# Graph-layer kernel: more gathered tiles replaced by column copies, and the copies spread over ScalarE and three places of VectorE's step

## The chip, the cores and the metric

The kernel runs on one core of one Trainium2 chip. The metric is device time in microseconds from start to end of one execution. The engines are TensorE (PE, with PEld for its weight loads), VectorE (DVE), ScalarE (ACT), GpSimd (POOL) and SyncE (SP). Each has its own in-order queue, and semaphores order them between each other. In the profile a name with a trailing q (DVEq, ACTq) stands for an instruction that the engine's queue handles itself, such as a load of registers.

## What is computed

The reference is one message-passing layer on a graph with 12,500 nodes (64 features each) and 200,000 edges (32 features each), sorted by destination, followed by a residual and a layer norm:

```python
msg_in = concatenate([x[src], x[dst], edge_attr_32], axis=-1)        # 200000 x 160
messages = relu(msg_in @ mW1 + mb1) @ mW2 + mb2                       # 160 -> 128 -> 64
aggregated = segment_sum(messages, dst, num_segments=12500)
upd = relu(concatenate([x, aggregated]) @ uW1 + ub1) @ uW2 + ub2      # 128 -> 128 -> 64
out = layernorm(x + upd)                                              # float32, no scale or shift
```

## The kernel before

The edges are cut into 1563 tiles of 128, and six tiles make a step, so there are 261 steps (`NSUB`). Two steps form a super-step `g` of 12 tiles. The product with `mW1` is split into three parts by the rows of the matrix. The part for `x[src]` is made once for all nodes: a table A of 12,500 rows of 128 numbers in DRAM (`tab_a`). For each tile POOL gathers the 128 rows that belong to its edges with one indirect DMA (L207, into `xg`). The part for `x[dst]` plus the bias is a second table B, of which 32 consecutive rows (a window) are enough for a tile because the edges are sorted. The part for the edge features is multiplied directly.

A step `s` of the main loop then runs like this:

- `edge_part(s)` on PE, already issued during step s - 1: for each tile one matmul (L363; two passes each, so twelve in the profile) of the left operand `l` (edge features, and a 0/1 matrix that picks the window's row) with `rhs` (weights and window rows), into the PSUM tile `pc`.
- `node_part(s)`: DVE adds the gathered rows, `h = pc + xg` (L390, or L386 for four tiles), and ACT takes the ReLU in place (L391, or L387 and L388).
- `collect(s - 1)` on PE: each tile's `h` is multiplied with a 0/1 matrix `sel` and summed into `sums` (L418), and a count of edges is kept (L423).
- In even steps `select(g + 1)`: DVE makes the 0/1 parts of the next super-step's `l` (L233, L235) and its `sel` (L239); SP then loads the edge features into `l` (`load`, L254), and ACT makes a bfloat16 copy of `sel` (`counts`, L247). In odd steps SP loads destinations (`loadd`).
- When a range of up to 448 nodes is complete, the step is an update. There are 33 of them, at steps that lie 47 apart at first and 4 apart at the end, since the later edges belong to more nodes. `close` copies the sums (ACT, L437 and L438), `update` multiplies (PE, L460 and L461) and ACT takes a ReLU with a bias (L462), `residual` multiplies again (PE, L469 and L470), DVE takes statistics (`bn_stats`, L474 and L476), ACT a square root with a bias (L478), and `norm`, at the start of the next step, lets DVE write the result (L484, L487), which SP stores. `pc`, `pu` and `py` share two PSUM slots.

The buffers for gathered rows form a ring of nine steps: POOL may gather a step as soon as DVE has added the rows of the step nine before it.

**Copied tiles.** In some steps (the list `COPIED`) the last two of six tiles are not gathered. The node features lie transposed in SBUF instead, one node in a column: `xtop` has them in its upper 64 partitions and zeros below, `xbot` the other way round. For 128 edges of each of the two tiles a tile `xc` of 128 x 128 is put together column by column: the upper half of column e is the source node of edge e of the first tile, the lower half that of the second. PE multiplies it with the weights (L366, four matmuls of 64 rows) on top of `pc`. Which column to copy is known only at run time, so registers are loaded with the column numbers (`values_load_multi_w_load_instructions`, a TENSOR_LOAD in the queue) and the copies address SBUF through them. `copies(s)` runs at the end of each step and makes a fourth of the `xc` that is needed two steps after the last fourth:

- ACT makes columns 0 to 63 (`SINGLE`), each with two copies of 64 partitions, upper and lower (L328, L330); 16 columns a step, after one load of 16 registers that hold two numbers each.
- DVE makes columns 64 to 127, each with one bitwise OR of an `xtop` and an `xbot` column (L341); 16 a step, after one load of 32 registers (L334).

`COPIED` is 20, 24, ..., 248. In the main loop of the kernel before, the part that matters here is in this order (what is left out stands between):

```python
node_part(s); collect(s - 1); close(...)
if j == 0 and g + 1 < NSUP:
    select(g + 1); load(g + 1); counts(g + 1)
...
update(...); edge_part(s + 1); residual(...)
rest(s)
copies(s)
```

Nothing reorders it: each engine's queue holds its instructions in the order in which this loop writes them.

Of the kernel before, what the change touches and what calls it, by code (L numbers as in the profile page):

```python
# [10 lines left out]
F32 = mybir.dt.float32  # L11
I32 = mybir.dt.int32
# [5 lines left out]
P = 128  # L18
# [53 lines left out]
YBASE = XBASE + 4 * XCOLS  # L72
FIRST, GAPS = 20, (4,)
COPIED = []
while FIRST + sum(GAPS) * (len(COPIED) // len(GAPS)) + sum(GAPS[:len(COPIED) % len(GAPS)]) < NSUB - 12:
    COPIED.append(FIRST + sum(GAPS) * (len(COPIED) // len(GAPS)) + sum(GAPS[:len(COPIED) % len(GAPS)]))
RNDS = -(-len(COPIED) // len(GAPS))
SINGLE = 64

# [19 lines left out]
def gnn_kernel(ctx: ExitStack, tc: tile.TileContext, x1T, x, eT, e_rows, src, src_row, dst, dst_row, wlist, wrow, wnext, whalf,  # L99
# [41 lines left out]
    cols = const.tile([RNDS * len(GAPS), 2 * P], I32, name="cols")  # L141
    col_i = const.tile([RNDS * len(GAPS), SINGLE, 2], U16, name="col_i")
    col_a = const.tile([RNDS * len(GAPS), P - SINGLE, 2], I32, name="col_a")
    w1b = const.tile([P, DH], F32, name="w1b")
# [67 lines left out]
    with tc.tile_pool(name="sup", bufs=2) as sup, tc.tile_pool(name="work", bufs=2) as work, tc.manual_schedule():  # L212
# [12 lines left out]

        def select(g):

# [6 lines left out]
            for r in ([slice(0, P)] if g > 2 else [slice(q, q + WIN) for q in SK]):  # L234
                nc.vector.tensor_tensor(l[r], l[r].bitcast(I32),  # L235
                                        node[r].unsqueeze(2).broadcast_to([r.stop - r.start, SUP // 2, P]),
                                        op=ALU.is_equal)
            s = sup.tile([P, SUP, WIN], F32, name="sel")
            nc.vector.tensor_tensor(s[:, :nt], slot.unsqueeze(1).broadcast_to([P, nt, WIN]),  # L239
# [46 lines left out]
        def columns_list():  # L286

            for r in range(len(GAPS)):
                v = src_row[:, ((FIRST + sum(GAPS[:r])) * SUB + SUB - 2) * P:]
                nc.sync.dma_start(cols[r * RNDS:(r + 1) * RNDS],  # L290
                                  bass.AP(v.tensor, v.offset, [[sum(GAPS) * SUB * P, RNDS], [1, 2 * P]]))
            cv = cols.rearrange("k (b e) -> k b e", b=2)
            iv = col_i.rearrange("k (b e) h -> k b e h", b=2)
            nc.vector.tensor_scalar(iv[:, :, :, 0], cv[:, :, :SINGLE:2], 4.0, float(XBASE), op0=ALU.mult, op1=ALU.add)
            nc.vector.tensor_copy(iv[:, :, :, 1], cv[:, :, 1:SINGLE:2])
            for b, base in enumerate((XBASE, YBASE)):
                nc.vector.tensor_scalar(col_a[:, :, b], cv[:, b, SINGLE:], 4.0, float(base), op0=ALU.mult, op1=ALU.add)

# [6 lines left out]

        def copies(s):

            for j, c in enumerate(COPIED):
                gap = GAPS[(j - 1) % len(GAPS)]
                if c - 2 - gap <= s < c - 2:  # L310
                    break
            else:
                return
            q = s - (c - 2 - gap)
            k = j % len(GAPS) * RNDS + j // len(GAPS)
            if q == 0:
                xc[c] = work.tile([P, P], F32, name="xc")
            o8 = xc[c].bitcast(U8)
            last_a = 4 * (N - 1)
            lo, hi = shares(SINGLE, gap, 4)[q]  # L320
            _, v = nc.values_load_multi_w_load_instructions(  # L321
                col_i.rearrange("k e b -> k (e b)").bitcast(I32)[k:k + 1, lo:hi], engines=[ET.Activation],
                min_val=0, max_val=N * 65536 - 1, skip_runtime_bounds_check_because="sources are node numbers")
            for i, w in zip(range(lo, hi), v):
                b, e = divmod(i, SINGLE // 2)
                o = o8[b * D:b * D + D, 8 * e:8 * e + 8]
                n = (w & 65535).with_bounds(min_val=XBASE, max_val=XBASE + last_a) - XBASE
                nc.scalar.copy(o[:, :4], x8[:D, bass.ds(n, 4)])  # L328
                n = (w >> 16).with_bounds(min_val=0, max_val=N - 1) * 4
                nc.scalar.copy(o[:, 4:], x8[:D, bass.ds(n, 4)])  # L330
            lo, hi = shares(P - SINGLE, gap, 2)[q]
            for a in range(lo, hi, 16):
                m = min(a + 16, hi)
                _, v = nc.values_load_multi_w_load_instructions(  # L334
                    col_a.rearrange("k e b -> k (e b)")[k:k + 1, 2 * a:2 * m], engines=[ET.DVE], min_val=XBASE,
                    max_val=YBASE + last_a, skip_runtime_bounds_check_because="sources are node numbers")
                for e in range(a, m):
                    i, n = (w.with_bounds(min_val=base, max_val=base + last_a) - base
                            for w, base in zip(v[2 * (e - a):], (XBASE, YBASE)))
                    w = 4 * (SINGLE + e)  # L340
                    nc.vector.tensor_tensor(o8[:, w:w + 4], x8[:, bass.ds(i, 4)], y8[:, bass.ds(n, 4)],  # L341
                                            op=ALU.bitwise_or)

# [384 lines left out]
        for s in range(last + 2):  # L728
# [8 lines left out]
            if s < NSUB:  # L737
                node_part(s)
            if 1 <= s <= NSUB:
                collect(s - 1)  # L740
            if s + 1 in due:
                close(due[s + 1])
            if j == 0 and g + 1 < NSUP:
                select(g + 1)
                load(g + 1)
                counts(g + 1)
# [16 lines left out]
            rest(s)  # L763
            copies(s)
            if s - 1 in due:
# [171 lines left out]
```

## Time and profile before

| | us |
|---|---|
| median of 3 runs (lowest, highest) | 1831.2 (1829.88, 1834.96) |
| profiled execution | 1832.05 |
| its span, first to last instruction | 1830.3 |
| mean granted TensorE clock | 0.577 of full speed |

| engine | busy us | share of the span | instructions |
|---|---|---|---|
| PE | 1440.8 | 79% | 9446 |
| DVE | 856.1 | 47% | 4895 |
| ACT | 1157.8 | 63% | 8032 |
| POOL | 1369.6 | 75% | 1456 |

Register loads, waits and other work of a queue do not count as busy, so an engine with a low share may still be unable to start anything else. A group of the profile gives the line, the engine, the operation, its operands, how often it ran, its busy time and the mean in ns of one; then the idle time of the engine just before these instructions and what ended it. "issue" is idle time in which nothing that the profile shows was awaited. Copies on ACT and DVE overlap their neighbours, so their mean is longer than the distance between two of them.

### The profile page before, as it was taken

What the parts mean: (1) busy time and instruction counts of PE and PEld (TensorE: products, weight loads), DVE (VectorE), ACT (ScalarE), POOL (GpSimd) and SP (SyncE); (2) the same over time, 40 slices, a digit from 0 to 9 for tenths busy, and PEclk for the clock granted to TensorE, in tenths of its full rate; (3) what the DMA queues carried; (4) which work ended last, traced back from release to release, by engine and by line L of the source; (5) the groups of instructions that cost most, each with busy time, mean ns of one, the idle gap of its engine ahead of it and who ended that gap; (6) DMA issues with size and microseconds to landing.
All of it is one profiled execution on the core that took longest, in us unless ns stands there. A gap on an engine that the chain in (4) does not pass through costs nothing.

```text
span 1830.3 us, 51040 instructions
## 1 busy us (share of the span) xinstructions
PE 1440.8 (79%) x9446; PEld 1243.3 (68%) x9446; DVE 856.1 (47%) x4895; ACT 1157.8 (63%) x8032; POOL 1369.6 (75%) x1456
## 2 busy tenths in 40 slices
PE   3697897776777777777877788887888888888887
PEld 3586887676666666666766667776766766767765
DVE  1565664454444444435444445444444544544432
ACT  0224886676676767757766667676776776767511
POOL 7777777777777777777777777777777777777774
PEclk8755655555555555555555555555556556566565
DMA  8874444333333333333333333433343433444432
GB/s 212 202 147 123 125 125 120 96 90 91 90 93 94 95 91 94 101 92 98 100 100 102 99 102 100 107 104 100 106 106 101 110 103 101 109 107 108 109 103 63
DMA packets 209512, 197.52 MB, mean 108 GB/s; under 512 B 58284, under 2 KB 174079, under 8 KB 209199
## 3 DMA queue, kind: packets, MB, share of 16 engines
q0 software_dynamic: 46304, 92.96, 20.4%
q1 hardware_dynamic: 148350, 92.34, 18.5%
q10 hardware_dynamic: 14546, 8.93, 1.8%
q8 instruction: 90, 1.47, 0.3%
q14 instruction: 222, 1.82, 0.3%
HBM read 176.40 MB, written 17.66 MB: 106 GB/s over the span
## 4 chain that ended last, share of the span: by engine, by line
POOL 36%; issue 23%; PE 19%; DMA 10%; DVE 7%; ACT 3%; ACTq 1%; DVEq 1%; SPq 1%; POOLq 0%
POOL xg L207 36%; PE sums L418 7%; DMA xg<-tab_a,src_s 5%; PE pc L363 4%; DVE xc L341 2%; PE pu L460 2%; PE pu L461 1%; DMA tab_a<-tb 1%; DMA l<-in_dst_row 1%; DVE h L390 1%; DVE l L235 1%; PE py L469 1%; PE py L470 1%; ACTq L321 1%; ACT xc L328 1%
## 5 line engine op out<-in xcount | busy, mean ns | idle before, releaser
L207 POOL DMA_INDIRECT xg<-tab_a,src_s x1387 | 1310.8, 945 | 422.7 <-issue 402.0
L418 PE MATMUL sums<-sel,h 128*128 128x32 f32 x3126 | 665.9, 381 | 191.7 <-ACT h L391 186.7
L418 PEld LDWEIGHTS sums<-sel,h 128*128 128x128 f32 x3126 | 635.5, 307 | 254.5 <-ACT h L391 228.8
L328 ACT COPY xc<-xtop 64x4 uint8 x3712 | 698.4, 188 | 114.1 <-issue 112.8
L330 ACT COPY xc<-xtop 64x4 uint8 x3712 | 714.4, 192 | 10.9 <-issue 10.9
L363 PE MATMUL pc<-rhs,l 64*128 64x128 f32 x3126 | 421.5, 424 | 134.8 <-DVE o L487 113.4
L363 PEld LDWEIGHTS pc<-rhs,l 64*128 64x128 f32 x3126 | 349.9, 305 | 191.7 <-DVE o L487 117.1
L341 DVE TENSOR_TENSOR xc<-xtop,xbot 128x4 uint8 x3712 | 299.6, 155 | 278.4 <-issue 278.1
L390 DVE TENSOR_TENSOR h<-pc,xg 128x768 f32<-128x768 f32 (+1 forms) x194 | 183.6, 947 | 355.5 <-DMA xg<-tab_a,src_s 263.4
L391 ACT ACTIVATE h<-h 128x768 f32<-128x768 f32 (+1 forms) x194 | 162.2, 837 | 245.9 <-DVE h L390 235.4
L235 DVE TENSOR_TENSOR l<-l,cps 128x768 f32<-128x768 int32 (+1 forms) x134 | 127.8, 954 | 29.4 <-DMA l<-in_dst_row 25.1
L247 ACT CAST selb<-sel 128x384 bf16<-128x384 f32 x131 | 66.1, 505 | 68.0 <-DVE sel L239 62.0
L474 DVE BATCH_NORM_STATS2 st<-py 128x6 f32<-128x64 f32 x131 | 20.5, 218 | 145.0 <-PE py L470 141.7
L423 PE MATMUL cnt<-selb,one 128*1 128x32 bf16 x1563 | 84.8, 188 | 0.0
L239 DVE TENSOR_TENSOR sel<-cps,drc 128x384 f32<-128x384 f32 x131 | 71.9, 549 | 20.2 <-PE sums L418 19.3
L478 ACT ACTIVATE sd<-mv,eps 128x4 f32<-128x4 f32 (+1 forms) x33 | 9.8, 297 | 109.4 <-DVE mv L476 109.4
L207 POOL DMA_INDIRECT xg<-in_x,src_s x60 | 57.7, 962 | 19.1 <-issue 18.0
L423 PEld LDWEIGHTS <-one 128*1 128x1 bf16 x1563 | 54.0, 83 | 22.5 <-issue 8.7
L386 DVE TENSOR_TENSOR h<-pc,xg 128x512 f32<-128x512 f32 x58 | 39.8, 686 | 49.4 <-DMA xg<-tab_a,src_s 29.5
L460 PE MATMUL pu<-sums_s,w2u 128*128 128x448 f32 (+1 forms) x66 | 61.2, 1032 | 0.5 <-ACT sums_s L437 0.5
L469 PE MATMUL py<-ux,xw 128*128 128x64 f32 x262 | 54.0, 289 | 5.1 <-ACT hTu L462 4.9
L470 PE MATMUL py<-u,hTu 128*128 128x64 f32 x262 | 52.5, 283 | 0.4 <-ACT hTu L462 0.4
(105 smaller groups left out, 857.3 us busy)
## 6 DMA issues: line engine op xcount, KB each, us to landing
l<-in_dst_row SPq DMA_DIRECT2D x262, 96.0 KB
l<-in_eT SPq DMA_DIRECT2D x262, 96.0 KB
xg<-tab_a,src_s POOLq DMA_INDIRECT x1387
rhs<-tab_b SPq DMA_DIRECT2D x361, 32.0 KB
tab_b<-tb SPq DMA_DIRECT2D x13, 512.0 KB
rhs<-tab_b SPq DMA_DIRECT2D x387, 16.0 KB
tab_a<-tb ACTq DMA_DIRECT2D x12, 512.0 KB
out<-o SPq DMA_DIRECT2D x32, 128.0 KB
```

Source lines behind the costliest of these rows:

```text
L207: nc.gpsimd.indirect_dma_start(out=a[:, i, :] if s < XG else a[:, i // 2, i % 2, :], out_offset=None, in_=A[:, :] if s >= XG else x[:, :], ...
L235: nc.vector.tensor_tensor(l[r], l[r].bitcast(I32), node[r].unsqueeze(2).broadcast_to([r.stop - r.start, SUP // 2, P]), op=ALU.is_equal)
L328: nc.scalar.copy(o[:, :4], x8[:D, bass.ds(n, 4)])
L330: nc.scalar.copy(o[:, 4:], x8[:D, bass.ds(n, 4)])
L341: nc.vector.tensor_tensor(o8[:, w:w + 4], x8[:, bass.ds(i, 4)], y8[:, bass.ds(n, 4)], op=ALU.bitwise_or)
L363: nc.tensor.matmul(pc[:, b, k, :], L[g][q:q + 64, m, :], rhs[g % 2][q:q + 64, w, :], start=s >= XG or k == 0, stop=s >= XG and not copied)
L390: nc.vector.tensor_tensor(h[:, b, :m], pc[:, b, :m], a[:, b, :m], op=ALU.add)
L391: nc.scalar.activation(h[:, b, :m], h[:, b, :m], AF.Relu)
L418: nc.tensor.matmul(ps[:, bass.ds(ws[i], WIN)], h[:, i % 2, i // 2, :], S[g][:, k0 + i, :], start=False, stop=ends and i == n - 1)
L423: nc.tensor.matmul(pn[:, bass.ds(ws[i], WIN)], one, SB[g][:, k0 + i, :], start=False, stop=ends and i == n - 1)
L460: nc.tensor.matmul(pu, w2u, sums_s[u % 2][:, :n], start=True, stop=False)
L469: nc.tensor.matmul(py[:, i], xw[u % 2][:, i * P:(i + 1) * P], ux, start=True, stop=False)
```

## The change

- `COPIED` becomes 16, 19, 22, 24, 27, 30, 32, ..., 254: three copied steps in eight instead of two, and to nearer the end.
- ACT makes columns 0 to 55 (`ACTS`), each with a single ACTIVATE that adds the `xbot` column, as a pointer bias, to the `xtop` column (`singly`); 20, 20 and 16 in the steps of a gap of three, 28 and 28 in a gap of two. It stands right behind `node_part`, ahead of the step's other ACT work.
- DVE makes columns 56 to 127, still with one OR each, now on one 4-byte word instead of four bytes (`joined`); 24 a step in a gap of three, 36 in a gap of two. A step's share is cut into places: two in odd steps (behind `node_part`, at the end), three in even steps (behind `node_part`, within `select` between L235 and L239, at the end). Each place loads its own registers, at most 32 at once.

```diff
--- before.py
+++ after.py
@@ -70,12 +70,13 @@
 XBASE = 8320
 U8, U16 = mybir.dt.uint8, mybir.dt.uint16
 YBASE = XBASE + 4 * XCOLS
-FIRST, GAPS = 20, (4,)
+FIRST, GAPS = 16, (3, 3, 2)
 COPIED = []
-while FIRST + sum(GAPS) * (len(COPIED) // len(GAPS)) + sum(GAPS[:len(COPIED) % len(GAPS)]) < NSUB - 12:
+while FIRST + sum(GAPS) * (len(COPIED) // len(GAPS)) + sum(GAPS[:len(COPIED) % len(GAPS)]) < NSUB - 6:
     COPIED.append(FIRST + sum(GAPS) * (len(COPIED) // len(GAPS)) + sum(GAPS[:len(COPIED) % len(GAPS)]))
 RNDS = -(-len(COPIED) // len(GAPS))
-SINGLE = 64
+LAST = 4 * (N - 1)
+ACTS = 56
 
 
 def updates():
@@ -139,8 +140,8 @@
     past = const.tile([1, 1], F32, name="past")
 
     cols = const.tile([RNDS * len(GAPS), 2 * P], I32, name="cols")
-    col_i = const.tile([RNDS * len(GAPS), SINGLE, 2], U16, name="col_i")
-    col_a = const.tile([RNDS * len(GAPS), P - SINGLE, 2], I32, name="col_a")
+    col_i = const.tile([RNDS * len(GAPS), ACTS, 2], U16, name="col_i")
+    col_a = const.tile([RNDS * len(GAPS), P - ACTS, 2], I32, name="col_a")
     w1b = const.tile([P, DH], F32, name="w1b")
     b1 = const.tile([P, DH], F32, name="b1")
 
@@ -223,7 +224,7 @@
                 nc.sync.dma_start(l[q:q + WIN].bitcast(I32), dv[:, b].broadcast_to([WIN, SUP // 2, P]))
             L[g] = l
 
-        def select(g):
+        def select(g, at=None):
 
 
             nt = min(SUP, NT - g * SUP)
@@ -235,6 +236,8 @@
                 nc.vector.tensor_tensor(l[r], l[r].bitcast(I32),
                                         node[r].unsqueeze(2).broadcast_to([r.stop - r.start, SUP // 2, P]),
                                         op=ALU.is_equal)
+            if at is not None:
+                joined(at, 1, 3)
             s = sup.tile([P, SUP, WIN], F32, name="sel")
             nc.vector.tensor_tensor(s[:, :nt], slot.unsqueeze(1).broadcast_to([P, nt, WIN]),
                                     drc[:, g * SUP:g * SUP + nt].unsqueeze(2).broadcast_to([P, nt, WIN]),
@@ -290,11 +293,10 @@
                 nc.sync.dma_start(cols[r * RNDS:(r + 1) * RNDS],
                                   bass.AP(v.tensor, v.offset, [[sum(GAPS) * SUB * P, RNDS], [1, 2 * P]]))
             cv = cols.rearrange("k (b e) -> k b e", b=2)
-            iv = col_i.rearrange("k (b e) h -> k b e h", b=2)
-            nc.vector.tensor_scalar(iv[:, :, :, 0], cv[:, :, :SINGLE:2], 4.0, float(XBASE), op0=ALU.mult, op1=ALU.add)
-            nc.vector.tensor_copy(iv[:, :, :, 1], cv[:, :, 1:SINGLE:2])
+            nc.vector.tensor_scalar(col_i[:, :, 0], cv[:, 0, :ACTS], 4.0, float(XBASE), op0=ALU.mult, op1=ALU.add)
+            nc.vector.tensor_copy(col_i[:, :, 1], cv[:, 1, :ACTS])
             for b, base in enumerate((XBASE, YBASE)):
-                nc.vector.tensor_scalar(col_a[:, :, b], cv[:, b, SINGLE:], 4.0, float(base), op0=ALU.mult, op1=ALU.add)
+                nc.vector.tensor_scalar(col_a[:, :, b], cv[:, b, ACTS:], 4.0, float(base), op0=ALU.mult, op1=ALU.add)
 
         x8, y8 = xtop.bitcast(U8), xbot.bitcast(U8)
 
@@ -303,43 +305,51 @@
             at = [-(-total * i // (n * of)) * of for i in range(n + 1)]
             return [(at[i], min(at[i + 1], total)) for i in range(n)]
 
-        def copies(s):
+        def portion(s):
 
             for j, c in enumerate(COPIED):
                 gap = GAPS[(j - 1) % len(GAPS)]
                 if c - 2 - gap <= s < c - 2:
-                    break
-            else:
+                    q = s - (c - 2 - gap)
+                    if c not in xc:
+                        xc[c] = work.tile([P, P], F32, name="xc")
+                    return xc[c], j % len(GAPS) * RNDS + j // len(GAPS), gap, q
+            return None
+
+        def singly(s):
+
+            if portion(s) is None:
                 return
-            q = s - (c - 2 - gap)
-            k = j % len(GAPS) * RNDS + j // len(GAPS)
-            if q == 0:
-                xc[c] = work.tile([P, P], F32, name="xc")
-            o8 = xc[c].bitcast(U8)
-            last_a = 4 * (N - 1)
-            lo, hi = shares(SINGLE, gap, 4)[q]
+            o, k, gap, q = portion(s)
+            lo, hi = shares(ACTS, gap, 4)[q]
             _, v = nc.values_load_multi_w_load_instructions(
                 col_i.rearrange("k e b -> k (e b)").bitcast(I32)[k:k + 1, lo:hi], engines=[ET.Activation],
                 min_val=0, max_val=N * 65536 - 1, skip_runtime_bounds_check_because="sources are node numbers")
-            for i, w in zip(range(lo, hi), v):
-                b, e = divmod(i, SINGLE // 2)
-                o = o8[b * D:b * D + D, 8 * e:8 * e + 8]
-                n = (w & 65535).with_bounds(min_val=XBASE, max_val=XBASE + last_a) - XBASE
-                nc.scalar.copy(o[:, :4], x8[:D, bass.ds(n, 4)])
-                n = (w >> 16).with_bounds(min_val=0, max_val=N - 1) * 4
-                nc.scalar.copy(o[:, 4:], x8[:D, bass.ds(n, 4)])
-            lo, hi = shares(P - SINGLE, gap, 2)[q]
+            for e, w in zip(range(lo, hi), v):
+                i = (w & 65535).with_bounds(min_val=XBASE, max_val=XBASE + LAST, guaranteed_mod_val=0, out_of_modulus=4)
+                n = (w >> 16).with_bounds(min_val=0, max_val=N - 1)
+                nc.scalar.activation(o[:, e:e + 1], x8[:, bass.ds(i - XBASE, 4)].bitcast(F32), AF.Identity,
+                                     bias=xbot[:, bass.ds(n, 1)])
+
+        def joined(s, part, of):
+
+            if portion(s) is None:
+                return
+            o, k, gap, q = portion(s)
+            lo, hi = shares(P - ACTS, gap, 2)[q]
+            n = -(-(hi - lo) // (2 * of)) * 2
+            lo, hi = lo + part * n, min(hi, lo + part * n + n)
             for a in range(lo, hi, 16):
                 m = min(a + 16, hi)
                 _, v = nc.values_load_multi_w_load_instructions(
                     col_a.rearrange("k e b -> k (e b)")[k:k + 1, 2 * a:2 * m], engines=[ET.DVE], min_val=XBASE,
-                    max_val=YBASE + last_a, skip_runtime_bounds_check_because="sources are node numbers")
+                    max_val=YBASE + LAST, skip_runtime_bounds_check_because="sources are node numbers")
                 for e in range(a, m):
-                    i, n = (w.with_bounds(min_val=base, max_val=base + last_a) - base
+                    i, n = (w.with_bounds(min_val=base, max_val=base + LAST, guaranteed_mod_val=0, out_of_modulus=4)
                             for w, base in zip(v[2 * (e - a):], (XBASE, YBASE)))
-                    w = 4 * (SINGLE + e)
-                    nc.vector.tensor_tensor(o8[:, w:w + 4], x8[:, bass.ds(i, 4)], y8[:, bass.ds(n, 4)],
-                                            op=ALU.bitwise_or)
+                    nc.vector.tensor_tensor(o[:, ACTS + e:ACTS + e + 1].bitcast(I32),
+                                            x8[:, bass.ds(i - XBASE, 4)].bitcast(I32),
+                                            y8[:, bass.ds(n - YBASE, 4)].bitcast(I32), op=ALU.bitwise_or)
 
         xc = {}
 
@@ -736,12 +746,14 @@
                 windows(s + 2)
             if s < NSUB:
                 node_part(s)
+                joined(s, 0, 3 if j == 0 and g + 1 < NSUP else 2)
+                singly(s)
             if 1 <= s <= NSUB:
                 collect(s - 1)
             if s + 1 in due:
                 close(due[s + 1])
             if j == 0 and g + 1 < NSUP:
-                select(g + 1)
+                select(g + 1, s)
                 load(g + 1)
                 counts(g + 1)
             if j == 1 and g + 2 < NSUP:
@@ -761,7 +773,7 @@
             if s + 2 in due:
                 columns(due[s + 2])
             rest(s)
-            copies(s)
+            joined(s, 2 if j == 0 and g + 1 < NSUP else 1, 3 if j == 0 and g + 1 < NSUP else 2)
             if s - 1 in due:
                 store(due[s - 1])
```

## Prediction

> **What bounds the kernel now.** I read the page first (busy shares, the chain that ended last), then the groups by line, then the waits of VectorE (DVE) and ScalarE (ACT), then the stretches of the span, and last the queue instructions that load registers. The page and the group of gathers:
>
> ```profile
> PE 1440.8 (79%) x9446; PEld 1243.3 (68%) x9446; DVE 856.1 (47%) x4895; ACT 1157.8 (63%) x8032; POOL 1369.6 (75%) x1456
> ...
> POOL 36%; issue 23%; PE 19%; DMA 10%; DVE 7%; ACT 3%; ACTq 1%; DVEq 1%; SPq 1%; POOLq 0%
> ...
> L207 POOL DMA_INDIRECT xg<-tab_a,src_s x1387 | 1310.8, 945 | 422.7 <-issue 402.0
> ```
>
> The gathers' own line (nanoseconds of the shortest, median and longest; first and last start):
>
> ```profile
> L207 POOL DMA_INDIRECT xg<-tab_a,src_s x1387: 940/944/1973, 78.9 to 1811.1; - x199
> ...
> L207 POOL DMA_INDIRECT xg<-in_x,src_s x60: 940/944/1578, 2.8 to 77.6; - x60
> ```
>
> POOL is busy only 75%, but its idle time is "issue": 0.30 us after each 0.945 us gather, with nothing awaited. The first of the 1447 gathers starts at 2.8 us and the last at 1811.1: (1811.1 - 2.8) / 1446 = 1.2506 us each, all the way through. The kernel is this train of gathers plus a tail of 19 us. The waits say the same from the other side: VectorE stands waiting for gathered rows, and POOL never waits for long. Waits of DVE and of ACT (total us, times, longest):
>
> ```profile
> DVE xc L341 <- issue: 278.1, 238, 2.1
> DVE h L390 <- DMA xg<-tab_a,src_s: 263.4, 87, 7.0
> DVE st L474 <- PE py L470: 141.7, 32, 9.5
> ...
> ACT xc L328 <- issue: 112.8, 235, 1.0
> ACT sd L478 <- DVE mv L476: 109.4, 33, 4.2
> ```
>
> The reader is to see that VectorE's slack is 263 + 30 us (h waiting for rows, in both forms of h), that each update costs VectorE 141.7/33 = 4.3 us of standing and ACT 109.4/33 = 3.3 us, and that 278 us go by before copies without a releaser. Those are register loads, which a queue does before the copies can be issued. The lines of the loads (one register in L769, 32 in L334, 16 in L321):
>
> ```profile
> L334 DVEq TENSOR_LOAD <-col_a x232: 2097/2152/2719, 159.8 to 1709.2; - x116
> ...
> L321 ACTq TENSOR_LOAD <-col_i x232: 1010/1034/1424, 158.2 to 1710.8; - x116
> ...
> L769 DVEq TENSOR_LOAD <-flag_i x1: 312/312/312, 1825.7 to 1825.7; - x1
> ```
>
> The one small ACTIVATE with a pointer bias, and the busiest stretch (busy us of PE, PEld, DVE, ACT, POOL, the clock, DMA):
>
> ```profile
> L478 ACT ACTIVATE sd<-mv,eps x33: 296/297/298, 362.3 to 1825.1; 128x4 f32<-128x4 f32 x32, 128x3 f32<-128x3 f32 x1
> ...
> 1500.00:1700.00 200.00, 167.22 (x1070) 139.09 (x1071) 98.86 (x628) 142.09 (x1006) 151.10 (x160) 0.62 0.40 107
> ```
>
> **POOL, the gain.** Copied steps go from 58 (20, 24, ... 248) to 90 (16, 19, 22, 24, ... 254). Each leaves out 2 gathers, so 64 gathers go: 64 x 1.2506 = 80.0 us. Eight steps take POOL 44 x 1.2506 = 55.0 us now and 42 x 1.2506 = 52.5 us after. All other engines must now do eight steps in 52.5 us, with three copied tile pairs to fill instead of two. If they do, the profiled execution's 1832.05 us (0.85 above the median of the three runs) becomes 1752.
>
> **PE.** The 32 more copied steps bring 4 matmuls L366 each, about 0.8 us a step in the timeline, 26 us in all. In the busiest stretch shown above PE is busy 167 of 200 us, 46.0 per eight steps; with one more copied step 46.8 of 52.5. It stays covered; uncovered it would cost the 26 us.
>
> **SP and the start.** The transfer of edge features into l (L254) waits for the comparison L235, which moves behind the first place of copies, so it starts some 1.7 us later in each even step, and what SP issues next with it. PE waited only 7.8 us for it in all, and the tile is needed at the end of the next step: I cost it at nothing; without that cover it would be 131 x 1.7 = 223 us of PE time, of which PE's idle 389 us would still take most. Copies begin at step 12 instead of 14; the x columns and the column numbers are there by step 10: nothing.
>
> **DVE per eight steps.** Now: busy 46% of 55.0 is 25.1, and the uncovered loads are 278.1/58 x 2 = 9.6, so 34.7 us. After: 3 x 72 = 216 copies instead of 128, 88 more at 81 ns (299.6 us / 3712): +7.1. The 22 loads are smaller but many. 32 registers cost 2.15 us, 1 costs 0.31, so 59 ns per register: 1.2 us for 8 columns, 1.7 for 12, 0.5 for 2 (the odd step with 36 columns has two places of 18, each 16 and a remainder of 2). A load runs in the queue while an earlier instruction executes: the add into h (0.95), the comparison into l (0.95), or the comparison into sel (0.55) with the copies still queued. This is what the new places bring: an even step's three loads follow h, l and sel each, instead of one long one after sel or h. Uncovered, after 0.09 us from a load's end to its first copy, I count about 1.0 us for an even step with 24 columns (three of these), 2.05 for an odd one (three), 2.6 and 4.0 for the even and odd step with 36: 15.8 us. The bounds are nothing and all 31.4 us of the loads; today 9.6 of 17.2, or 56%, is uncovered, and 15.8 of 31.4 is 50%. Sum 34.7 - 9.6 + 7.1 + 15.8 = 48.0, in which about 1.2 updates with 2.3 us of work each are contained. As a formula with n updates per eight steps, their 4.3 us of standing included: 45.2 + 6.6 n.
>
> **ACT per eight steps.** Each column was two 64-partition copies; they last 188 to 193 ns and start 105 ns apart, overlapping. A column is now one ACTIVATE with a pointer bias. The nearest row is L478: 297 ns for 4 elements with a pointer bias. The trace does not show such instructions back to back. If they overlap by the same 94 ns as copies do where the queue is ahead, a column costs 0.20 us; the bounds are 0.105 (as a copy) and 0.297 (no overlap). I take 0.20, because every pair of ACT operations in the timeline that had its operands early overlaps by about 0.09 (h of L387 lasts 0.62 and L388 starts 0.53 after it). 168 columns x 0.20 = 33.6; uncovered loads 6.3 (today 0.53 each; then 20, 20, 16 or 28, 28 registers instead of 16); h 7.2 and selb 2.0; per update 2.0 of work and 3.3 of standing. Together 49.1 + 5.3 n, less some 1.6 for overlaps between these: 47.5 + 5.3 n. No table loads are added: the changed program has the same two.
>
> [...]
>
> **Where the gain is given back.** POOL's 52.5 is met by DVE up to n = 1.1 and by ACT up to n = 0.95. Updates become denser along the list of edges: the first come at steps 47, 66, 81, from step 150 they are 5 to 7 apart, at the end 4. From 150 to 252 there are 20, n = 1.57: DVE 55.6, ACT 55.8, about 3.2 too much, over 12.75 periods 40 us. These are not two losses: both stand in the same chain of an update (pu on PE, hTu on ACT, py on PE, bn_stats on DVE, sd on ACT, norm on DVE). What is late there is hTu: L462 is queued behind ACT's copies of the step, where today it stands ahead of them, and PE's py, DVE's bn_stats with the copies behind it, and the next h all wait for it. VectorE reaches bn_stats later than before, since one or two of its places of copies lie ahead of it, so I take the old 4.3 us; if hTu comes 2 us later than that, 20 updates cost 40 more; if the ring of nine row buffers (9 x 6.5 = 59 us) and the uncopied last steps take the lag up, nothing is lost. Before step 150 the gain stays.
>
> Forecast: 1832 - 80 + 40 = 1792. Its own range is 1765 (almost all absorbed) to 1825 (80 lost).
>
> **Rivals.** *POOL remains the only bound* and the lag is taken up whole: 1752 to 1765. For it: 293 us of VectorE waiting for rows that vanish first. Against it: the sums above leave nothing over late. Chance 0.11.
>
> *All is given back*, by a later hTu as priced and some uncovered PE: 1826 to 1837. Chance 0.08.
>
> *ACT becomes the bound and it gets slower.* The mechanism is the pointer bias: if the read of xbot's column does not run under the instruction before it, ACT's period grows with 168 columns. Averaged over the kernel (n = 33/30 = 1.1) ACT needs 47.5 + 5.8 + 168 (p - 0.20) per eight steps; it reaches today's 55.0 at p = 0.21. At 0.23 it is 58.3, and 30 periods x 3.3 give 1832 + 99 = 1931; at 0.297 it is 69.6 and about 2270. The price I took is only 0.01 below the turning point. For it: L478's 297 ns, and that ACT then never waits for DVE. Against: the overlap seen in every other ACT pair. Chance 0.25.
>
> [...]
>
> *The change does not do what it says*, the copies staying at a step's end: the changed instruction order shows them in their places, so I give it nothing.
>
> **Numbers.** The likeliest is the forecast, 0.56 over 1765 to 1825. Less than 0.3% (5.5 us) can't be told from no change. Faster by more: 0.56 + 0.11 = 0.67; within: 0.08; slower: 0.25. The range goes from 1762 to 1862: it leaves out most of the first rival and the dearer half of the ACT rival, some 0.2 together.
>
> **What would show each step.** Right: 1383 gathers still 1.25 us apart up to about step 150 (by there 17 copied steps more, some 43 us ahead of today), then gaps in POOL released by VectorE; VectorE's wait for rows falling from 263 to under 60 us; ACTIVATEs of xc starting about 0.20 us apart; register loads on DVE of 1.2 and 1.7 us with little idle time before the copies of even steps; st still waiting about 4 us for py. Wrong: ACTIVATEs of xc 0.23 us or more apart with POOL waiting from the first hundred steps on (slower), or POOL without gaps to the end (nearer 1755); also PE waiting long for l or xc, which no term above holds.

## The result: 4.4% slower, and the profile after

| | us |
|---|---|
| kernel before, median of 4 runs (lowest, highest) | 1830.54 (1829.39, 1834.96) |
| changed kernel, median of 4 runs (lowest, highest) | 1911.75 (1906.08, 1914.21) |
| ratio, 95% interval | 1.0436 (1.0416 to 1.0456) |
| changed kernel, profiled execution and its span | 1912.23, 1910.3 |

A later pair of runs of the same changed kernel beside the kernel before gave 1912.66 against 1831.11, ratio 1.0447 (1.0417 to 1.0477). The earlier runs that its expectation speaks of, in which the kernel before took some 2830 us, are told in the last section:

> The changed kernel itself, as the reference for the runs so far: in their calls the kernel before took 2822 to 2842 us instead of 1831. If the kernel before is back at 1831, this gives 1912. If it is still at about 2830, it gives the changed kernel's time under those conditions: by theory 1 (close behind ACT's columns delays updates) it lies at least 30 us above the 2996 of e1_close_first; by rival 2 within 15 us of it; and if ACT's instructions are what binds there, e4_no_bias (2681) and e2_act_end (2880) lie far below it.

The page of the changed kernel, its engine line, the chain that ended last and the group of gathers:

```profile
PE 1483.7 (78%) x9574; PEld 1276.2 (67%) x9574; DVE 1057.1 (55%) x7663; ACT 1349.1 (71%) x5680; POOL 1309.0 (69%) x1392
...
issue 26%; ACTq 16%; PE 14%; ACT 13%; DVE 12%; POOL 9%; DMA 2%; DVEq 2%; POOLq 0%
...
L208 POOL DMA_INDIRECT xg<-tab_a,src_s x1323 | 1250.3, 945 | 516.5 <-issue 367.4
```

The gathers are 64 fewer (1387 before) and last as long as before, so POOL's work has shrunk as planned. But POOL's share of the chain has fallen from 36% to 9%. What ends last is now spread over ACT, its queue, DVE and PE, and 26% of it is "issue", time in which nothing that the profile shows was awaited. Where POOL lost its hold is seen in the stretches of the changed kernel (busy us of PE, PEld, DVE, ACT, POOL, the clock, DMA):

```profile
700.00:1100.00 400.00, 318.97 (x1969) 274.97 (x1968) 226.30 (x1756) 308.51 (x1329) 302.47 (x321) 0.53 0.36 98
1100.00:1500.00 400.00, 314.62 (x1860) 265.42 (x1860) 212.56 (x1651) 286.55 (x1226) 261.50 (x278) 0.54 0.34 91
...
1500.00:1700.00 200.00, 149.24 (x922) 123.37 (x922) 105.23 (x817) 142.76 (x605) 125.87 (x135) 0.57 0.33 90
```

Up to 1100 us POOL issues 321 gathers in 400 us, which is the old 1.25 us each. In the next stretch it is down to 278, and in the last to 135 of the 160 that the kernel before issues there. PE's busy time in that last stretch has fallen too, from 167 to 149 us, and ACT's is the same as before (142.8 and 142.1). So no engine is busy throughout. But the idle time of DVE between 1100 and 1500 us has only two sources of any size:

```profile
DVE xc L350 <- issue: 100.0, 126, 2.1
DVE st L484 <- PE py L480: 84.1, 9, 11.5
```

DVE works for 212.6 us, stands 100.0 before copies for their register loads (the records of the loads lie under 88 of it) and 84.1 for `py` in nine updates, together 396.7 of the 400 us. It has no time left over, so what it stands longer in an update makes the step longer. The waits of the changed kernel over the whole span (total us, times, longest):

```profile
DVE xc L350 <- issue: 461.2, 592, 2.4
...
DVE st L484 <- PE py L480: 287.1, 33, 11.6
ACT xc L331 <- issue: 148.7, 298, 1.5
ACT sd L488 <- DVE mv L486: 126.5, 33, 6.1
...
PE cnt L431 <- ACT xw L448: 86.3, 30, 4.7
...
POOL xg L208 <- DVE h L400: 60.0, 19, 7.8
POOL xg L208 <- DVE h L396: 56.6, 16, 9.0
...
ACT hTu L472 <- PE pu L471: 21.7, 26, 2.6
```

DVE no longer waits for gathered rows (263 us in h before). Instead it stands for `py` in every update: 287.1/33 = 8.7 us against 4.3. The profile of the later pair, of the same kernel, has 270.1, or 8.2 per update, so half a microsecond per update means nothing below. A wait that the kernel before did not have is PE's for `xw`, 86.3/30 = 2.9 us per update. POOL now waits for DVE to free rows.

The step-by-step times (the start of PE's first L428, or L418 before, of a step, changed less before) show when this cost arrives: +4 us at step 50, -12 at 80, -7 at 150, then +28 at 200, +88 at 250 and +79 at the last step. POOL's last gather of step 150 was issued 45 us earlier than before (1008.0 against 1052.8), but PE's work on that step was only 7 us ahead (0.2 in the profile of the later pair). The rest of the gain stood in the ring as rows that nobody had taken yet: the distance from a step's last gather to PE's work on it was 5 to 12 us before (from step 50 on); in the changed kernel it is 45 us at step 150 and 51 to 76 from step 170 on, which is the ring full. After the start, POOL's first gap is at the gathers of step 177 (1187.6 us). After the last gather 66 us follow, where 19 did.

One update of the changed kernel, from its timeline (start us, us, engine, line, operation, in brackets the idle time before and its releaser):

```profile
1554.55 0.54 ACT L447 COPY sums_s<-sums 128x480 f32<-128x480 f32 x1
...
1554.99 0.54 ACT L448 COPY xw<-cnt 1x480 f32<-1x480 f32 x1
...
1555.58 0.56 PE L431 MATMUL cnt<-zero_b 128*1 128x480 bf16 x1 [2.66 <-ACT xw L448]
...
1556.23 3.06 ACT L331 ACTIVATE xc<-xtop,xbot 128x1 f32 x16
...
1560.94 0.63 ACT L472 ACTIVATE hTu<-pu,ub_s 128x448 f32<-128x448 f32 x1 [1.25 <-PE pu L471]
...
1563.96 0.63 DVE L484 BATCH_NORM_STATS2 st<-py 128x6 f32<-128x64 f32 x4 [8.17 <-PE py L480]
...
1564.91 0.30 ACT L488 ACTIVATE sd<-mv,eps 128x4 f32<-128x4 f32 x1 [3.33 <-DVE mv L486]
...
1567.78 1.46 PE L373 MATMUL pc<-rhs,l 64*128 64x128 f32 x12 [2.31 <-DVE o L497]
1568.69 0.84 ACT L401 ACTIVATE h<-h 128x768 f32<-128x768 f32 x1 [3.48 <-DVE h L400]
```

ACT copies the sums (L447, L448) only when the columns of that step are done (the last 14 take 2.85 us from 1551.79 on); PE stands 2.66 us for it, and everything behind PE's `cnt` moves with it. Then ACT makes the next step's columns (L331, 3.06 us), which stand ahead of `hTu`. DVE stands 8.17 us, ACT 3.33 and then 3.48, PE 2.31. `hTu` itself does not wait for its columns here (it has 1.25 us left over), because `pu` is late already. That is why the two places had to be tested separately and together.

### The profile page after: what moved, and what is told of

It is laid out like the page before. It is cut to its first block, busy times and chain, and to the rows that moved or that the text cites. A ratio compares the mean times of both kernels' runs of the same rounds, so it can differ in the third digit from the quotient of the medians.

```text
span 1910.3 us, 54714 instructions
## 1 busy us (share of the span) xinstructions
PE 1483.7 (78%) x9574; PEld 1276.2 (67%) x9574; DVE 1057.1 (55%) x7663; ACT 1349.1 (71%) x5680; POOL 1309.0 (69%) x1392
## 4 chain that ended last, share of the span: by engine, by line
issue 26%; ACTq 16%; PE 14%; ACT 13%; DVE 12%; POOL 9%; DMA 2%; DVEq 2%; POOLq 0%
ACTq L331 11%; POOL xg L208 9%; ACT xc L331 8%; ACTq L325 5%; DVE xc L350 5%; ACT h L401 3%; PE pc L373 2%; PE pu L470 2%; PE pu L471 2%; DVEq L344 2%; DMA xg<-tab_a,src_s 2%; PE py L479 2%; DVE h L400 2%; PE py L480 2%; PE sums L428 1%
## 5 line engine op out<-in xcount | busy, mean ns | idle before, releaser
L208 POOL DMA_INDIRECT xg<-tab_a,src_s x1323 | 1250.3, 945 | 516.5 <-issue 367.4
L331 ACT ACTIVATE xc<-xtop,xbot 128x1 f32 x5040 | 1021.1, 290 | 150.6 <-issue 148.7
L350 DVE TENSOR_TENSOR xc<-xtop,xbot 128x1 int32 x6480 | 520.6, 154 | 463.4 <-issue 461.2
L428 PE MATMUL sums<-sel,h 128*128 128x32 f32 x3126 | 666.2, 382 | 142.1 <-ACT h L397 71.6
L428 PEld LDWEIGHTS sums<-sel,h 128*128 128x128 f32 x3126 | 637.4, 308 | 202.4 <-ACT h L401 99.1
L401 ACT ACTIVATE h<-h 128x768 f32<-128x768 f32 x162 | 134.3, 830 | 113.4 <-DVE h L400 106.0
L484 DVE BATCH_NORM_STATS2 st<-py 128x6 f32<-128x64 f32 x131 | 20.5, 219 | 287.1 <-PE py L480 287.1
L400 DVE TENSOR_TENSOR h<-pc,xg 128x768 f32<-128x768 f32 x162 | 152.6, 943 | 6.7 <-PE pc L373 5.2
L431 PE MATMUL cnt<-zero_b 128*1 128x480 bf16 x33 | 18.2, 553 | 86.3 <-ACT xw L448 86.3
L397 ACT ACTIVATE h<-h 128x512 f32<-128x512 f32 x90 | 55.7, 619 | 39.8 <-DVE h L396 39.7
L376 PE MATMUL pc<-w1a,xc 64*128 64x128 f32 x360 | 72.3, 404 | 0.0
L396 DVE TENSOR_TENSOR h<-pc,xg 128x512 f32<-128x512 f32 x90 | 61.6, 685 | 5.8 <-PE pc L376 4.5
L376 PEld LDWEIGHTS pc<-w1a,xc 64*128 64x128 f32 x360 | 64.7, 318 | 0.0
```

The source lines that it names most:

```text
L208: nc.gpsimd.indirect_dma_start(out=a[:, i, :] if s < XG else a[:, i // 2, i % 2, :], out_offset=None, in_=A[:, :] if s >= XG else x[:, :], ...
L331: nc.scalar.activation(o[:, e:e + 1], x8[:, bass.ds(i - XBASE, 4)].bitcast(F32), AF.Identity, bias=xbot[:, bass.ds(n, 1)])
L350: nc.vector.tensor_tensor(o[:, ACTS + e:ACTS + e + 1].bitcast(I32), x8[:, bass.ds(i - XBASE, 4)].bitcast(I32), y8[:, bass.ds(n - YBASE, 4) ...
L376: nc.tensor.matmul(pc[:, b, k, :], xc[s][q:q + 64], w1a[q:q + 64], start=False, stop=True)
L400: nc.vector.tensor_tensor(h[:, b, :m], pc[:, b, :m], a[:, b, :m], op=ALU.add)
L401: nc.scalar.activation(h[:, b, :m], h[:, b, :m], AF.Relu)
```

## The experiments

The theory after the result: *place*. ACT's columns stand ahead of two links of the update's chain on ACT, `close` (L447, L448, in the step before the update) and `hTu` (L472, in the update's step). Rivals: *ACT's total*, the columns being too much work wherever they stand; *DVE's places*, its copies now standing ahead of the chain; *DVE's total*. All ratios are to the kernel before, with 95% intervals. The rates quoted are us per eight steps over steps 150 to 198 and 198 to 250, where 1.33 and 1.85 updates fall into eight steps; the changed kernel has 60.8 and 64.5, the kernel before 55.3 and 55.0, and POOL with three copied steps in eight needs 52.5.

**Columns behind `close` in the step before an update.**

```diff
-                singly(s)
+                if s + 1 not in due:
+                    singly(s)
...
             if s + 1 in due:
                 close(due[s + 1])
+                if s < NSUB:
+                    singly(s)
```

> The changed kernel, but in the 33 steps in which close copies a finished range's sums (sums_s, xw), ACT's columns of xc are issued behind close instead of ahead of it; nothing else moves. Theory 1 (an update starts late because close stands behind ACT's columns): VectorE's standing for py falls from 287 us to about 170, PE's wait of the counts' opening matmul for xw (86 us) nearly vanishes, and the time falls from 1912 to about 1850. Rival 2 (hTu behind ACT's columns is the late link, as the prediction had it): py standing stays above 250 and the time above 1895. Rival 3 (ACT and DVE have too much work per step, wherever it stands): the time changes by less than 20 us although the xw wait goes.

1898.79 us (1892.92 and 1904.66), ratio 1.0366 (1.0289 to 1.0444): 14 us less than the changed kernel, where *place* at this one link was to give about 1850 with `st` near 170. Its waits:

```profile
DVE st L484 <- PE py L480: 258.6, 32, 11.6
...
PE py L479 <- ACT hTu L472: 77.3, 30, 6.2
```

The wait for `xw` (86.3) is gone, and 77.3 us of waiting for `hTu` have come in its place. The link freed was no longer late; the next link on the same engine was. Time and `st` are those that the expectation gave to rival 2, in which `hTu` is the late link.

**Columns behind the update's `hTu` alone.**

```diff
-                singly(s)
+                if s not in due:
+                    singly(s)
...
                 update(due[s])
+                if s < NSUB:
+                    singly(s)
```

> The changed kernel with ACT's columns moved behind hTu in the update's own step only; in the step before it they still stand ahead of close. If the second point is what costs (as the prediction named it): 1912 - 90 = about 1822. If the two points only pay together, each hiding the other: about 1895, as with the first alone (1899).

1914.67 us (1910.84 and 1918.51), ratio 1.046 (1.0439 to 1.048): no better than the changed kernel, so `hTu` alone is not the late link either. The 1822 of this one point did not come; the other forecast, that the points pay only together, fits within 20 us.

```profile
DVE st L484 <- PE py L480: 275.5, 33, 11.8
...
ACT hTu L472 <- PE pu L471: 114.7, 33, 4.4
...
PE cnt L431 <- ACT xw L448: 80.4, 28, 4.7
```

Now ACT is ready for `hTu` early and stands 114.7 us for `pu`, because `xw` is still late (80.4 us).

**Both.**

```diff
-                singly(s)
+                if s + 1 not in due and s not in due:
+                    singly(s)
...
                 close(due[s + 1])
+                if s < NSUB:
+                    singly(s)
...
                 update(due[s])
+                if s < NSUB:
+                    singly(s)
```

> The changed kernel, but around each update ACT's columns stand aside: in the step before it behind close, in the update's own step behind hTu; in all other steps they stay where the change put them. If the delay in the update's chain is the cause (theory 1, both points): an update costs about 6.6 us instead of 9.6 per eight steps' count, 20 updates after step 150 and some before it give 60 us back, about 1850. If ACT's total work per step binds (rival 3): above 1890, as with only the first point moved (1899).

1807.85 us (1807.78 and 1807.92), ratio 0.9875 (0.9853 to 0.9896). The four cells are 1912.7 (neither), 1898.8, 1914.7 and 1807.9: -14 and +2 alone, where runs of one kernel lie up to 12 us apart, and -105 together, with the same number of columns on ACT and of copies on DVE. The expectation of about 1850 counted 60 us; by the step-by-step times 26 of the 105 us come before step 150 and 79 behind it. Its stretch from 1100 us, and its waits:

```profile
1100.00:1500.00 400.00, 326.29 (x2065) 276.13 (x2065) 234.37 (x1817) 312.38 (x1337) 302.44 (x321) 0.57 0.39 103
```

```profile
DVE xc L350 <- issue: 460.6, 591, 2.4
...
DVE st L484 <- PE py L480: 151.6, 32, 11.6
...
ACT hTu L472 <- PE pu L471: 31.5, 22, 2.6
```

POOL is back at 321 gathers in 400 us up to 1500, and DVE stands 4.6 us per update for `py`, near the 4.3 of the kernel before. ACT is busier than in the changed kernel (312 against 287 us of 400): it was not full there. Where no update is near, ACT is full: in both kernels eight steps without an update (steps 54 to 62, 70 to 78) take 46.4 us, and from 388.1 to 434.5 us, such a stretch of the changed kernel, ACT idles 4.4 us, all of it before columns. That is 6 us below POOL's 52.5 and so costs nothing.

**All columns of ACT at the step's end**, behind `rest(s)`:

```diff
-                singly(s)
...
             rest(s)
+            singly(s)
```

> The changed kernel with all of ACT's columns moved to the end of the step, behind close, selb, hTu and sd, where the copies of the kernel before stood; DVE's three places stay. Theory 1: py standing about 150 us as in the kernel before (141.7), 1835 to 1850. Rival 2 gives the same here, and differs in the run before. Rival 3: above 1890, with the waits moved to ACT's h.

1916.0 us, ratio 1.046 (1.043 to 1.0491), neither the 1835 to 1850 of *place* nor `st` near 150. `st` waits less (220.6), but the columns are now ahead of the next step's ReLU, and PE waits for it twice as long as in the changed kernel (there 68.2 and 71.6 us):

```profile
PE sums L428 <- ACT h L401: 174.0, 89, 6.5
...
PE sums L428 <- ACT h L397: 115.5, 69, 3.6
```

In steps 14 to 46, which have no update, eight steps take 54.3 us against 49.2 in the changed kernel; from 198 to 250, where updates are dense, 61.2 against 64.5. So the place behind `node_part` is the better one where no update is near; only around updates it is the wrong one. Taken alone, this run is what the expectation gave to *ACT's total*; the run with both moves, with the same columns on ACT, is what excludes it.

**Half the work of a column.** The column is a plain copy instead of an addition with a pointer bias, which leaves out the second tile's features in 56 columns:

```diff
-                nc.scalar.activation(o[:, e:e + 1], x8[:, bass.ds(i - XBASE, 4)].bitcast(F32), AF.Identity,
-                                     bias=xbot[:, bass.ds(n, 1)])
+                nc.scalar.copy(o[:, e:e + 1], x8[:, bass.ds(i - XBASE, 4)].bitcast(F32))
```

> The changed kernel with ACT's columns made by a plain copy of the xtop column, without the bias (the second tile's source features of 56 columns are left out), same number and places. An instruction then starts about 0.105 us after its neighbour instead of 0.197, some 15.5 us less ACT time per eight steps. Theory 1 and rival 3 both: close comes about 2 us earlier in each update and ACT is free, 1790 to 1830. If DVE's work is what binds: above 1880.

The columns now start 0.093 us apart instead of 0.197. 1808.28 us, ratio 0.9872 (0.9844 to 0.9901). `st` waits 158.7 us, as in the run with both moves. Shorter columns in the wrong place and full columns in the right place come to the same time within 0.5 us. That the times agree so closely may be chance. This run alone would have fitted *ACT's total* as well as *place*, and the expectation gave both the same range; it is the run with both moves, with all of ACT's work, that excludes the first.

**Less on ACT, more on DVE** (48 columns on ACT instead of 56):

```diff
-ACTS = 56
+ACTS = 48
```

> The changed kernel with 48 columns on ACT and 80 on DVE. Per eight steps ACT has 24 columns x 0.197 = 4.7 us less, DVE 24 more at 0.07 and larger loads, about 4 us more. Rival 3 (ACT's work binds): 30 x 4.7 x the bound two thirds, 1830 to 1860. Theory 1: ACT's columns ahead of close and hTu are 0.5 us shorter each, some 20 us: about 1890. If DVE's work binds: 1930 or more.

1935.4 us, ratio 1.0571 (1.0549 to 1.0594). Taking work off ACT makes it slower. `st` falls to 179.3, but ACT now stands longer for DVE's h (205.9 us against 106.0 in the changed kernel):

```profile
DVE xc L350 <- issue: 526.0, 565, 2.2
...
ACT h L401 <- DVE h L400: 205.9, 131, 7.7
```

This is the time that the expectation gave to DVE's work (1930 or more). DVE has nothing to spare: eight copies more per tile, 24 in eight steps, and their loads cost more than ACT's relief brought; eight steps without an update take 49.2 us instead of 46.4. So *DVE's total* is not out. It is the sum to which the standing for `py` adds; place decides the standing.

**All DVE copies at the step's end**, the two other places taken out:

```diff
-            if at is not None:
-                joined(at, 1, 3)
...
-                joined(s, 0, 3 if j == 0 and g + 1 < NSUP else 2)
...
-            joined(s, 2 if j == 0 and g + 1 < NSUP else 1, 3 if j == 0 and g + 1 < NSUP else 2)
+            joined(s, 0, 1)
```

> The changed kernel with all of DVE's columns in one place at the end of each step (24 or 36, in loads of at most 32 registers); ACT as in the changed kernel. The prediction's count of uncovered loads gives the three places about 7 us per eight steps where engines bind: about 1912 + 60. If the places hide nothing: 1912 within 10. If the columns ahead of select and bn_stats themselves delay the chain: below 1890.

2015.51 us, ratio 1.1009 (1.0985 to 1.1032), 103 us above the changed kernel, where 60 was expected. `st` waits 323.6 us, and POOL 104.9 for `cps` alone. The three places are a good part of the change, and *DVE's places* is out as the reason for the loss. But they do not pay by what they were made for: eight steps without an update take 46.4 us here too (54 to 62, 70 to 78), so the whole loss falls around updates (59.1 us from 94 to 150, 69.1 from 198 to 250). Which of the places matters there was not run.

**Two copied steps in eight instead of three**, all else as changed:

```diff
-FIRST, GAPS = 16, (3, 3, 2)
+FIRST, GAPS = 20, (4,)
```

> The changed kernel with two tiles copied in every fourth step again (20, 24, ... 252: 59 copied steps, one more than before), so ACT makes 14 columns and DVE 18 a step; the new places, the joining on ACT and 56 of 128 columns on ACT stay. POOL needs 1445 gathers x 1.25 = 1807 us plus the tail. Theory 1 (delay of each update behind ACT's columns, hidden as long as the engines have room): POOL remains the bound, 1825 to 1832. If an update's delay alone is enough to bind, without the denser columns: above 1850.

1828.12 us (8 runs, 1826.47 to 1829.13), ratio 0.9984 (0.9973 to 0.9995). The new way of making columns costs nothing where POOL is the bound; it takes the third copied step in eight to bring the update's chain onto the path. The 2.5 us below the kernel before are the two gathers of the one copied step more.

**Dense copies only where updates are rare**, columns where the change put them (gaps 3, 3, 2 from step 16 to 112, 3 to 166, 4 to 254; 77 copied steps, 38 gathers fewer than before; the list is made from this line):

```diff
-FIRST, GAPS = 16, (3, 3, 2)
+PARTS = [(16, (3, 3, 2), 112), (112, (3,), 166), (166, (4,), 255)]
```

> The changed kernel with copied steps dense where updates are rare and sparse where they are frequent: gaps 3, 3, 2 from step 16 to 112, 3 to 166, 4 to 254; 77 copied steps, 19 more than before, 38 gathers fewer. By the fitted rates (fixed part 47 us at three copied steps in eight, about 43 at gap 3 and 35 at gap 4, plus 9.6 per update) the engines stay at or below POOL's pace throughout: 1831 - 38 x 1.25 = 1783, up to 1795 with some lag. If the changed places cost something wherever copying is dense, 1810 or more.

1784.25 us (1782.84 to 1785.12), ratio 0.9743 (0.9726 to 0.9761). 1831 - 38 x 1.2506 = 1783: every gather left out is paid in full. `st` still stands 224.0 us in it, and POOL's pace hides that.

**Both together, in two densities.** Columns moved around updates, with gaps 3, 3, 2 up to step 118, 3 to 192, then 3 and 4 in turn (81 copied, 46 gathers fewer), and gaps 3, 3, 2 up to 157, then 3 to 253 (86 copied, 56 fewer):

```diff
-FIRST, GAPS = 16, (3, 3, 2)
+PARTS = [(16, (3, 3, 2), 120), (120, (3,), 194), (195, (4, 3), 255)]
```

> The same with gaps 3, 3, 2 to step 118, 3 to 192, then 3, 4, 3 in turn to the end: some 82 copied steps, 48 gathers fewer, so 1771 if POOL is the bound all the way. It is faster than the denser one only if that one lags by more than 10 us at its end.

```diff
-FIRST, GAPS = 16, (3, 3, 2)
+PARTS = [(16, (3, 3, 2), 160), (160, (3,), 255)]
```

> ACT's columns stand aside as in the dodge run, gaps 3, 3, 2 from step 16 to 157 and 3 to 253: 86 copied steps, 28 more than before, 56 gathers fewer. With dodge's rates (about 44.5 us + 4.8 per update at gap 3 against POOL's 53.3) the engines keep up nearly to the end: 1831 - 56 x 1.25 = 1761, up to 1775 with lag. If an update still costs 9.6 at gap 3: above 1790.

1773.14 us (1772.82 to 1774.27), ratio 0.9687 (0.9674 to 0.97), which is 1831 - 46 x 1.2506 = 1773; and 1764.03 us (1762.38 to 1767.32), ratio 0.9639 (0.9626 to 0.9652), against 1761 by the same sum. The second is the fastest kernel of this study, 3.6% below the kernel before. The stretches of that second kernel:

```profile
1100.00:1500.00 400.00, 346.43 (x2194) 294.47 (x2191) 240.62 (x1770) 307.45 (x1292) 302.45 (x321) 0.58 0.38 106
1500.00:1700.00 200.00, 173.44 (x1115) 143.72 (x1114) 117.89 (x846) 149.06 (x617) 151.21 (x161) 0.62 0.39 109
```

POOL keeps 1.25 us a gather through both, and its gathers are the bound once more.

## Why the prediction was wrong

The forecast was 1792 and the time 1911.75, on the other side. Step by step:

- **POOL, right as far as it bound.** 64 gathers fewer, 1.25 us apart, then gaps released by DVE's h, as written, though the first came later (1187.6 us, gathers of step 177) than the "about step 150" of the forecast. The runs with 38 and 46 gathers fewer paid 1.25 us for each.
- **ACT's price of a column, right.** The line of the columns in the changed kernel:

```profile
L331 ACTq ALU_OP  x5040: 35/35/49, 132.4 to 1846.4; - x194
L331 ACTq FUSED_REGOPS  x5040: 63/67/83, 132.4 to 1846.5; - x194
L331 ACT ACTIVATE xc<-xtop,xbot x5040: 277/290/297, 132.6 to 1846.6; 128x1 f32 x194
```

  They last 290 ns and mostly start 0.185 to 0.201 us apart (median 0.197; 0.20 predicted). The rival in which ACT's price turns the sign needed over 0.21 and is out, although its sign came true. Each column starts 290 - 197 = 93 ns before the end of the one ahead of it, where the prediction took 94 over from the copies.
- **DVE's loads, right in size.** Uncovered loads were counted at 15.8 us per eight steps; 461.2/90 x 3 = 15.4 were measured. For ACT 6.3 were counted and 148.7/90 x 3 = 5.0 measured. The reason given, that the three places cover loads, is not borne out: with all copies in one place it is 513.6/90 x 3 = 17.1, only 1.7 more, so the size was in part luck.

```profile
L344 DVEq TENSOR_LOAD <-col_a x660: 340/1598/3344, 124.9 to 1842.4; - x165
```

- **The step that failed: "so I take the old 4.3 us".** The standing for `py` per update is 287.1/33 = 8.7 us. The prediction saw that `hTu` is queued behind ACT's columns and gave a possible later `hTu` 2 us and 40 us in all, outside the forecast. It did not see `close`: its two copies stand behind the columns of the step before the update, PE stands 86.3 us for `xw`, and no term held that. With DVE's own formula and only the standing s exchanged, 45.2 + (2.3 + s) n, the rates of four kernels come out to about 1 us. The price of one update, 2.3 + s by the formula, can also be measured without it: eight steps without an update take 46.4 us in all four kernels (54 to 62, 70 to 78), eight with one (62 to 70, 78 to 86, 86 to 94) take longer by the mean in the third column.

| kernel | s = st wait/33 | one update: formula, measured | n = 1.33: formula, measured | n = 1.85: formula, measured |
|---|---|---|---|---|
| changed | 8.7 | 11.0, 10.0 | 59.8, 60.8 | 65.6, 64.5 |
| behind `close` alone | 7.8 | 10.1, 8.9 | 58.6, 59.6 | 63.9, 63.3 |
| behind `hTu` alone | 8.3 | 10.6, 10.2 | 59.3, 60.1 | 64.8, 64.6 |
| both | 4.6 | 6.9, 6.5 | 54.4, 55.4 | 58.0, 57.4 |

  So the term that was mis-sized is the price of an update: 6.6 us forecast, about 10 measured, and 6.5 with the columns out of the chain's way. Then the old standing nearly holds (4.6), and so nearly does the forecast (1807.9). The fixed part was 1.2 us too low (45.2 against 46.4). Its 46% is DVE's share between 300 and 1100 us, where 0.76 updates fall into eight steps and not the 1.2 taken off; the page's 856.1 of 1830.3 us with 33 updates in 261 steps would have given 46.3.
- **"Before step 150 the gain stays": wrong.** POOL's gathers were 45 us ahead there, but PE's step only 7. Steps 94 to 150, with 0.86 updates per eight steps, already took 55.4 us against 52.5, and what POOL had won went into the ring. By the time updates became dense, 45 us of the ring's 51 to 76 were taken. The two misses together explain the number, as an estimate: 20 updates at 8.7 - 4.3 = 4.4 us are 88, and 43 - 7 = 36 us of the lead at step 150 were not there; 1792 + 88 + 36 = 1916, against 1911.75.
- **PE and SP at nothing: right for SP.** Waits of PE for `l` went from 7.8 to 20.1 us, small beside the rest. PE is not full, but it is a link of the chain and stands there.

With the columns moved, eight steps still grow with n: 53.4, 55.4 and 57.4 us at n = 0.86, 1.33 and 1.85. 46.4 + 6.5 n gives 52.0, 55.1 and 58.4, so most of this is the price of an update as forecast. Not settled: how much of the 4.6 us for which `st` still stands in an update could be saved. No run took a link off DVE.

## What to carry to other kernels

Filler work that nothing waits for soon was not free here (1912 us with the columns ahead of the two links of each update, 1808 with them behind), since ACT ran its instructions in the order written: put such work behind its engine's links of any chain that goes through several engines, and walk the whole chain for links on that engine, as freeing one of two moved the wait (-14 and +2 us) and freeing both paid 105. Do so only in the steps in which the chain runs: at the end of every step the same filler held up the next step's ReLU and gained nothing (1916 us). Price such a chain by what is queued ahead of each link in the changed order, not by its standing before. And spread filler by where the bound engine is ahead: dense where the chain is rare, thin where it is frequent.

## What the hardware showed beyond that

- A load of registers ran in the queue while earlier instructions executed, and about half of it was hidden: the 660 loads of DVE take 919 us together, a median of 1.60 each, and DVE's copies stood 461.2 us for them in all, 0.70 us a load.
- DVE's copies of 128x1 through registers start 70 ns apart with 152 ns of duration (73 apart and 154 long before, on bytes), so one 4-byte word instead of four bytes brought almost nothing.
- In three earlier sets of runs, of which none is used above, the kernel before took 2823 to 2842 us instead of 1831. The changed kernel itself was not run in them. With the columns behind `close` alone it took 2996 and 3004 us (medians of two runs each), with all of ACT's columns at the end 2880, with all of DVE's copies at the end 3001, with plain copies 2681 and with two copied steps in eight 2789. In the trace of the kernel at 2996 us, queue instructions on ACT that compute a column's address took up to 1.65 us, where the lines above have 0.083 at most, and the columns stood 1027 us for the queue instead of 148.7; with plain copies they stood 909 us, instead of 176.7 in the run of 1808 us above. What brings this about is open.
